# A graph-attention kernel: four weight tiles masked on GpSimd within the attention, and the first half of its output added to x there

## The chip, the core and the metric

The kernel runs on one core of a Trainium2 chip. A core has five engines that each work through a queue of their own in program order and wait for each other through semaphores: TensorE (PE in the profile, with PEld for its weight loads), VectorE (DVE), ScalarE (ACT), GpSimd (POOL) and SyncE (SP), which here only issues transfers. Matrix products are written to PSUM, everything else lies in SBUF. The metric is the device time of one execution in microseconds; the lower, the better.

## What is computed

Two graph layers over x of 16 batches x 1024 nodes x 256 channels, in fp32. Cut to what matters:

```python
# layer 0
h = relu(layernorm(x))
c_adj = mean(h, channels)                     # one number per node
diff = c_adj[:, None, :] - c_adj[:, :, None]
A = abs(abs(sigmoid(diff) - 0.5) - 0.5) * 2
W = adj * (A + A^T) / 2                       # 1024 x 1024 weights of each batch
q = relu((h^T W) * para)                      # the "graph" product
k, v = split(h @ kv_w)
x = x + softmax(q k^T * scale) v              # 4 heads of 64
# layer 1
h = relu(layernorm(x))
x = x + batchnorm(relu(batchnorm((A_hat h) @ W1.T + b1)) @ W2.T + b2)
```

A_hat is the adjacency matrix with unit diagonal added, normalized by its degrees. The batch norms run over all batches and nodes, so layer 1 is finished only when all 16 batches have passed its first product.

## The kernel before

The batches go one after another. While batch b is in its attention, the graph weights W of batch b+1 are begun; then the rest of them is made beside the graph product of b+1, then the values and keys of b+1 are made, and then the first product of layer 1 runs for batch b. That is one turn of the loop at L1440; the order of all instructions of PE, ACT, DVE, POOL and SP is the order in which the code issues them (`manual_schedule`, L1366), so each engine's queue is written by hand.

**Weights.** W of a batch is made in 8 tiles of 128 x 1024, one for 128 nodes. `differences` (L350) is two ScalarE instructions: the absolute difference (L353) and its tanh (L356). `masked` (L359) is one VectorE instruction (L361): (w - 1) times the tile of adj. The sign that this leaves is taken up in the scale of the queries. `weights` is both. The tiles live in a pool of five buffers (`w4`), tile 7 elsewhere.

**Attention** (`attention`, L791) goes in four steps: two halves g of 512 queries, and for each two pairs of heads. A step is `scores` (for 8 blocks m of keys: products into PSUM at L802, the exponential by ScalarE at L810, and the sums of exponentials by VectorE at L816, L822 and L825, with an odd and an even partial sum that L830 adds), then `partial` (VectorE: a transpose at L836 and a reduction at L844), then `values` (products at L852 and VectorE's transpose of their result at L865). In `scores`, the steps in `before_last` are issued ahead of L830; `hooks` puts `weights` of tiles 0 and 1 of the next batch there, in steps 0 and 1.

**Finishing a half** (`finish`, L870) has five parts: `collect` (ScalarE copies, L879), `invert` (VectorE: reciprocals of the sums, L885 to L888), `spread` (ScalarE copies, L894), `scale` (VectorE multiplies the half's output by them, L903, and 16 transfers on SP's queue put it into the order of x, L920) and `add` (VectorE adds it to x, L928). Half 0 is complete after step 1: its `collect` stands within step 2, `invert` and `spread` ahead of L830 of step 2, `scale` behind `partial` of step 2. Its `add` and all five parts of half 1 are returned in a list, `left`, and issued later.

**The graph stage** (`graph_seven`, L501; for batch 1 `graph`, L385) makes the graph product of b+1. Tiles 0 and 1 are multiplied plainly (L514). Tiles 2 to 7 are taken in three pairs, by seven products of sums of blocks in place of eight products (L575, `m1` to `m_7`), whose sums VectorE makes (`make_t1` to `make_t4`, L555 to L568). The stage begins with `differences` of tiles 2, 3 and 4, `masked` of 2 and 3, and `collect` and `invert` of the half 1 of batch b; masks 4 to 7 follow between the products. The add of half 0 (`add0`) stands behind the last sums, at L660, and the layer norm of the first half of x (`norm.stats(0, 4)`) behind it. The add of half 1 (`add1`, L746) comes in the values and keys stage.

In the first turn `between` (L1460) issues the list, with the add of half 0 behind tile 2's mask. In the last turn there is no next batch: `left[:3]` (the add, `collect`, `invert`) follows the attention at L1545, ahead of the first product of layer 1 for batch 14, which multiplies blocks of A_hat by h and by sums of blocks of h that VectorE makes at L995 to L998 (`sums_of_h`).

Of the kernel before, what the change touches and what calls it, by code (L numbers as in the profile page):

```python
# [10 lines left out]
F32 = mybir.dt.float32  # L11
AF = mybir.ActivationFunctionType
# [17 lines left out]
def fast_path(  # L30
# [145 lines left out]
    with ExitStack() as stage:  # L176
# [173 lines left out]
        def differences(b, c, w=None):  # L350
            if w is None:
                w = w4.tile([P, N], F32, tag="w4", name=f"f_w_{b}_{c}")
            nc.scalar.activation(  # L353
                w, rows[b], AF.Abs, bias=cols[b][:, c : c + 1], scale=0.5 / C
            )
            nc.scalar.activation(w, w, AF.Tanh)  # L356
            ws[b, c] = w

        def masked(b, c):  # L359
            w = ws[b, c]  # L360
            nc.vector.scalar_tensor_tensor(w, w, 1.0, adj_t[c], ALU.subtract, ALU.mult)  # L361
# [139 lines left out]
        def graph_seven(b, left, norm, load_more, last):  # L501
# [2 lines left out]


            gps = [ps_s.tile([P, N], F32, tag="s", name=f"f_gps_{b}_{d}") for d in range(CC)]
            add0, collect, invert, spread, scale, add1 = left
            h = hs[b]

            def plain(c):  # L510
# [91 lines left out]
            def m_7(n):  # L602
                one(m7, s3[n], t3[n], n, False, True)

            differences(b, 2)
            differences(b, 3)
            differences(b, 4)
            masked(b, 2)
            masked(b, 3)
            collect()  # L610
            invert()
            masked(b, 4)
# [44 lines left out]
            for n in range(PAIRS):  # L657
                m5(n)
            nc.scalar.copy(room[:, 1], x)
            add0()  # L660
            norm.stats(0, 4)
            norm.invert(0, 4)
            nc.vector.tensor_add(room[:, 2], room[:, 2], m7)
# [124 lines left out]
                todo.insert(0, late)  # L788
            return (qT, kT, v), todo

        def attention(b, qT, kT, v, hooks):  # L791

            steps = [(g, pair) for g in range(NH) for pair in range(HEADS // 2)]
            p_of, acc_of, odd_of, oT_of, o_of, red_of = {}, {}, {}, {}, {}, {}

            def scores(s, within=None, before_last=()):
                g, pair = steps[s]
                for m in range(NC):
                    ps = ps_s.tile([P, 2, 512], F32, tag="s", name=f"f_s_{b}_{s}_{m}")
                    for e in range(2):  # L800
                        rows_e = slice(e * HD, (e + 1) * HD)
                        nc.tensor.matmul(  # L802
                            ps[:, e, :],
                            kT[rows_e, pair, ts(m, P)],
                            qT[rows_e, pair, ts(g, 512)],
                            start=True,
                            stop=True,
                        )
                    p = pp.tile([P, 2, 512], F32, tag="p", name=f"f_p_{b}_{s}_{m}")
                    nc.scalar.activation(p, ps, AF.Exp)  # L810
                    p_of[s, m] = p
                    if m == 1:
                        acc = pp.tile(
                            [P, 2, 512], F32, tag="acc", name=f"f_acc_{b}_{s}", bufs=2
                        )
                        nc.vector.tensor_add(acc, p_of[s, 0], p)  # L816
                        acc_of[s] = acc
                    elif m == 3:
                        odd = ow.tile([P, 2, 16, 32], F32, tag="sums", name=f"f_sums_{b}_{s}")
                        odd_of[s] = odd  # L820
                        flat = odd.rearrange("p e j i -> p e (j i)")
                        nc.vector.tensor_add(flat, p_of[s, 2], p)  # L822
                    elif m > 3:
                        to = flat if m % 2 else acc_of[s]
                        nc.vector.tensor_add(to, to, p)  # L825
                    if m == 5 and within:
                        within()
                for step in before_last:
                    step()
                nc.vector.tensor_add(acc_of[s], acc_of[s], flat)  # L830

            def partial(s):

# [102 lines left out]
            for i in range(len(steps)):  # L936
                scores(
                    i,
                    collect if i == 2 else None,
                    [*hooks.get(i, ()), *([invert, spread] if i == 2 else [])],  # L940
                )
                partial(i)
                if i == 2:
                    scale()
                values(i)
            return [add] + finish(1)

# [416 lines left out]
        with tc.manual_schedule(engines={ENG.PE, ENG.Activation, ENG.DVE, ENG.Pool, ENG.SP}):  # L1366
# [72 lines left out]
            diagonal()  # L1439
            for b in range(B):  # L1440

                hooks = {}
                if b + 1 < B:
                    for c in range(2):
                        hooks.setdefault(c, []).append(lambda c=c: weights(b + 1, c))
                    if b == 0:
                        for m in range(NC):
                            hooks.setdefault(m // 2, []).append(lambda m=m: column_sums(m))
                        hooks[3].append(roots)
                else:  # L1450
                    hooks[0] = [lambda norm=norm: norm.relu(4, NC, False)]
                    w2n = lasting.tile([P, CC, F1], F32, tag="w2n", name="f_w2n")
                    nc.sync.dma_start(w2n, W2.rearrange("(c p) f -> p c f", p=P))
                left = attention(b, *qkv, hooks)

                def more(c):
                    return lambda: weights(b + 1, c)
# [1 line left out]
                norm = Norm(xr[b], f"b{b}")  # L1459
                between = {  # L1460
                    0: [
                        lambda: turn_h(b + 1), more(2), left[0], left[1], left[2], more(3),
                        left[3], left[4], more(4),
                    ],
                    1: [more(5)],
                    2: [more(6), lambda: norm.stats(0, 4)],
                    3: [more(7)],
                    4: [left[5], lambda: norm.stats(4, NC), norm.invert],
                    6: [lambda: norm.relu(0, 4)],
                    "late": [lambda: norm.relu(4, 6), lambda: norm.relu(6, NC)],  # L1470
                    8: [lambda: leave(b), lambda: arrive(b + 2)],
# [22 lines left out]
                if b + 2 < B:  # L1494
                    made = None
                    if b > 0:
                        made = sums_of_h(b, norm.h)
                        todo.pop(0)()
                    linear1_all(
                        b,  # L1500
                        norm.h,
                        thirds,
                        lambda: ([step() for step in todo], prepare_start(b + 2)),
                        lambda: (prepare_end(b + 2), pair_sums(b + 2, 0, 2)),
                        lambda: (prepare_row(b + 2), again(b + 1)),
                        turning=lambda: (pair_sums(b + 2, 2, 3), turn_h_aside(b + 2)),
                        made=made,
                    )
                elif b + 1 < B:
                    kept_h = norm.h  # L1510
                    again(b + 1)
                else:

                    w2T = lasting.tile([P, FC, C], F32, tag="w2T", name="f_w2T")

                    def first():
                        norm.stats(0, 4)
                        norm.invert(0, 4)
                        left[3]()
                        left[4]()  # L1520

                    def second():
                        norm.shifts(0, 4)
                        norm.relu(0, 4, False)

                    def third():
                        left[5]()
                        norm.stats(4, NC)
                        norm.invert(4, NC)
                        for n, (pool, tag) in enumerate(((ps_o, "o"), (ps_t, "t"))):  # L1530
                            ps = pool.tile([P, 2, CC, P], F32, tag=tag, name=f"f_w2ps_{n}")
                            for d in range(2):
                                for f in range(CC):
                                    nc.tensor.transpose(
                                        ps[:, d, f, :], w2n[:, f, ts(2 * n + d, P)], ident
                                    )
                            nc.scalar.copy(
                                w2T[:, 2 * n : 2 * n + 2, :].rearrange("p d c -> p (d c)"),
                                ps.rearrange("p d f q -> p (d f q)"),
                            )  # L1540
                        norm.shifts(4, NC)
                        norm.relu(4, NC, False)
                        leave(b)

                    for step in left[:3]:  # L1545
                        step()
                    thirds = load_thirds(b)
                    def nothing():
                        pass

                    made = []
                    linear1_all(
                        b - 1,
                        kept_h,
                        thirds,
                        first,
                        second,
                        third,
                        lambda: made.extend(sums_of_h(b, norm.h)),
                    )  # L1560
                    linear1_all(b, norm.h, thirds, nothing, nothing, nothing, made=made)
# [882 lines left out]
```

## Time and profile before

| | |
|---|---|
| time, median of 3 runs | 2384.4 us (2383.52 to 2384.42) |
| the profiled execution's own time | 2382.97 us |
| its span in the profile | 2381.1 us |
| TensorE's granted clock, mean | 0.995 |
| one batch in the middle (850.9 to 981.2 us) | 130.3 us |
| of it: attention; graph stage; values and keys; layer 1 | 56.3; 25.1; 12.9; 36.0 us |
| VectorE: mask of a tile (L361); add of a half (L928) | 1.21; 1.22 us |
| ScalarE: difference (L353); tanh (L356) | 1.16; 1.06 us |
| GpSimd: busy over the span | 175.1 us (7%) |

The span is the time from the first to the last instruction in the profile. An engine's row of the timeline gives start and length of an instruction, its line in the kernel, the tile that it writes and the tiles that it reads, and in brackets how long the engine had been idle before it and what ended that. Instructions of one engine can overlap a little at their ends: a VectorE addition of 1.22 us is followed by the next one 1.14 us after its start. Times in a trace are those of one execution, and sums made from them are held against its span.

### The profile page before, as it was taken

The numbers are of one execution on the slowest core, as the hardware profiler recorded it, in microseconds if no ns is written. First come the engines' busy times: TensorE is split into PE (matmuls) and PEld (weight loads), VectorE is DVE, ScalarE is ACT, GpSimd is POOL, SyncE is SP. The second block draws the span as 40 slices with busy tenths as digits, with TensorE's granted clock in tenths as the row PEclk, the third lists the DMA queues.
The fourth block names the chain that finished last, engine by engine and source line by source line (L and its number), as shares of the span: only waits on it lengthen the run. The fifth ranks groups of instructions, "written<-read, shape, count | busy, mean of one in ns | idle before, by whom it ended". The sixth has DMA issues, their size and how long they took to land.

```text
span 2381.1 us, 25131 instructions
## 1 busy us (share of the span) xinstructions
PE 2343.5 (98%) x8286; PEld 1037.3 (44%) x8286; DVE 1989.6 (84%) x2866; ACT 1352.6 (57%) x2002; POOL 175.1 (7%) x253
## 2 busy tenths in 40 slices
PE   8999999999999999999999999999999999999996
PEld 4443444434343434444343434344444434444444
DVE  6888989797989899897979798998979798757766
ACT  6846556464746555565647374555555575346654
POOL 2030010101010000101010100001010100000000
PEclk9999999999999999999999999999999999999998
DMA  5043433432342424334333414243433321355569
GB/s 194 8 145 93 147 119 129 137 122 91 97 160 68 167 93 169 97 129 137 124 98 110 146 62 169 89 172 93 146 120 127 114 92 53 114 203 188 175 238 381
DMA packets 178651, 316.40 MB, mean 133 GB/s; under 512 B 33616, under 2 KB 117072, under 8 KB 178512
## 3 DMA queue, kind: packets, MB, share of 16 engines
q1 hardware_dynamic: 164176, 271.18, 33.7%
q0 software_dynamic: 9728, 26.76, 3.8%
q10 hardware_dynamic: 4608, 16.78, 1.7%
q8 instruction: 67, 1.10, 0.2%
q14 instruction: 72, 0.59, 0.1%
HBM read 198.71 MB, written 97.05 MB: 124 GB/s over the span
## 4 chain that ended last, share of the span: by engine, by line
PE 97%; DVE 1%; DMA 1%; ACT 0%; issue 0%; SPq 0%; DVEq 0%; ACTq 0%; POOLq 0%; POOL 0%
PE f_s L802 19%; PE f_o L852 19%; PE f_aps L1011 16%; PE f_zps L1118 6%; PE f_gps L575 6%; PE f_gpsx L575 5%; PE f_gps L514 4%; PE f_zx L1661 4%; PE f_zm L1661 3%; PE f_gps L404 2%; PE f_kpsx L712 2%; PE f_vpsx L717 2%; PE f_vps L717 2%; PE f_kps L712 1%; PE f_z2ps L1599 1%; PE f_outps L1884 1%
## 5 line engine op out<-in xcount | busy, mean ns | idle before, releaser
L810 ACT ACTIVATE f_p<-f_s 128x1024 f32<-128x1024 f32 x512 | 477.5, 1048 | 189.2 <-PE f_s L802 189.1
L802 PE MATMUL f_s<-f_qT,f_kT 64*128 64x512 f32 x2048 | 457.3, 596 | 0.1
L852 PE MATMUL f_o<-f_p,f_v 128*64 128x512 f32 x2048 | 453.6, 595 | 0.0
L802 PEld LDWEIGHTS f_s<-f_qT,f_kT 64*128 64x128 f32 x2048 | 190.2, 185 | 264.8 <-ACT f_p L810 117.9
L852 PEld LDWEIGHTS f_o<-f_p,f_v 128*64 128x64 f32 x2048 | 141.4, 137 | 304.3 <-issue 265.4
L353 ACT ACTIVATE f_w<-f_row,f_col 128x1024 f32<-128x1024 f32 x127 | 147.0, 1157 | 40.0 <-PE f_gps L514 26.8
L825 DVE TENSOR_TENSOR f_acc<-f_acc,f_p 128x1024 f32<-128x1024 f32 x128 | 155.9, 1218 | 4.5 <-ACT f_p L810 4.5
L361 DVE SCALAR_TENSOR_TENSOR f_w<-f_w,f_adj 128x1024 f32<-128x1024 f32 x127 | 152.8, 1213 | 7.5 <-ACT f_w L356 7.2
L825 DVE TENSOR_TENSOR f_sums<-f_sums,f_p 128x1024 f32<-128x1024 f32 x128 | 155.8, 1217 | 0.0
L260 POOL TENSOR_TENSOR f_rstd_b<-f_var_b,f_mhalf 128x4 f32<-128x4 f32 (+1 forms) x31 | 33.1, 1069 | 1483.0 <-DVE f_var_b L259 1483.0
L356 ACT ACTIVATE f_w<-f_w 128x1024 f32<-128x1024 f32 x127 | 134.4, 1058 | 4.0
L1011 PE MATMUL f_aps<-f_ahatT,f_hs 128*128 128x512 f32 x256 | 115.1, 592 | 0.0
L1011 PE MATMUL f_aps<-f_ahatT,f_h_b 128*128 128x512 f32 x256 | 112.7, 593 | 0.0
L1011 PE MATMUL f_aps<-f_t,f_hs 128*128 128x512 f32 x256 | 112.5, 592 | 0.0
L816 DVE TENSOR_TENSOR f_acc<-f_p,f_p 128x1024 f32<-128x1024 f32 x64 | 76.9, 1201 | 27.6 <-ACT f_p L810 27.5
L514 PE MATMUL f_gps<-f_w,f_h_a 128*128 128x512 f32 x224 | 99.9, 599 | 0.0
L822 DVE TENSOR_TENSOR f_sums<-f_p,f_p 128x1024 f32<-128x1024 f32 x64 | 78.3, 1223 | 21.8 <-ACT f_p L810 21.8
L281 ACT ACTIVATE f_h_a<-f_x,f_shift_a,f_rstd_a 128x256 f32<-128x256 f32 x126 | 73.8, 587 | 38.5 <-DVE f_shift_a L266 38.5
L836 DVE STREAM_TRANSPOSE f_sums<-f_acc 128x1024 f32<-128x1024 f32 x64 | 79.7, 1245 | 2.2
L281 ACT ACTIVATE f_h_b<-f_x,f_shift_b,f_rstd_b 128x256 f32<-128x256 f32 x128 | 69.3, 595 | 21.5 <-DVE f_shift_b L266 21.5
L575 PE MATMUL f_gps<-f_w,f_h_a 128*128 128x512 f32 x168 | 81.2, 592 | 0.0
L1141 ACT ACTIVATE f_z<-f_zps,f_b 128x512 f32<-128x512 f32 x60 | 38.0, 683 | 75.3 <-PE f_zps L1118 75.3
(285 smaller groups left out, 3754.0 us busy)
## 6 DMA issues: line engine op xcount, KB each, us to landing
f_t<-ft SPq DMA_DIRECT2D x84, 512.0 KB, 11.1
fz<-f_z SPq DMA_DIRECT2D x64, 512.0 KB, 9.7
f_x<-in_x_dram SPq DMA_DIRECT2D x31, 1024.0 KB, 7.0
f_zb<-fz SPq DMA_DIRECT2D x42, 512.0 KB, 3.9
f_att<-f_oT SPq DMA_DIRECT2D x512, 32.0 KB, 1.9
fx<-f_x SPq DMA_DIRECT2D x16, 1024.0 KB, 4.4
fhT<-f_hQ POOLq DMA_DIRECT2D x112, 128.0 KB, 2.9
f_hT<-fhT SPq DMA_DIRECT2D x28, 512.0 KB, 5.9
```

The lines of the kernel that those rows point to most:

```text
L281: nc.scalar.activation(self.h[:, c, :], self.xt[:, c, :], AF.Relu, bias=self.shift[:, c : c + 1], scale=self.rstd[:, c : c + 1], accum_out ...
L353: nc.scalar.activation(w, rows[b], AF.Abs, bias=cols[b][:, c : c + 1], scale=0.5 / C)
L361: nc.vector.scalar_tensor_tensor(w, w, 1.0, adj_t[c], ALU.subtract, ALU.mult)
L514: nc.tensor.matmul(gps[d][:, ts(g, 512)], h[:, c, ts(d, P)], w[:, ts(g, 512)], start=(c == 0), stop=(c == PLAIN - 1),)
L575: nc.tensor.matmul(ps, left, right, start=fresh and n == 0, stop=(n == PAIRS - 1), skip_group_check=more,)
L802: nc.tensor.matmul(ps[:, e, :], kT[rows_e, pair, ts(m, P)], qT[rows_e, pair, ts(g, 512)], start=True, stop=True,)
L810: nc.scalar.activation(p, ps, AF.Exp)
L825: nc.vector.tensor_add(to, to, p)
L852: nc.tensor.matmul(o_of[s][e * HD : (e + 1) * HD, :], v[:, m, ts(2 * pair + e, HD)], p[:, e, :], start=(m == 0), stop=(m == NC - 1),)
L1011: nc.tensor.matmul(ps, left[:, m, :], right(m), start=not more and m == 0, stop=(m == KH - 1), skip_group_check=more,)
L1118: nc.tensor.matmul(ps[i], left[:, ts(i, P)], right, start=not more, stop=True, skip_group_check=more,)
L1661: nc.tensor.matmul(ps, left[:, m, :], right[:, m, :], start=start and m == 0, stop=(m == 1), skip_group_check=not start,)
```

## The change

Three things are done, all in the attention and the stages behind it.

From the second turn on, `differences` of tiles 0 to 3 of the next batch are issued in steps 0 to 3 of the attention (before: `weights` of 0 and 1 in steps 0 and 1, and `differences` of 2 and 3 in the graph stage). Their masks are made by a new function, `masked_aside`, which is issued behind L830 of the same step: VectorE sets a column to -1, ScalarE adds it to the tile, and GpSimd multiplies the tile by that of adj. `masked(b, 2)` and `masked(b, 3)` go from the graph stage. The first turn keeps its way of making tiles 0 and 1.

In every turn, the add of half 0 is issued in step 3 of the attention, ahead of L830 and of that step's hooks. It goes from the graph stage, from `between` and from the end of the last turn.

```diff
+        def masked_aside(b, c):
+            now = small.tile([P, 1], F32, tag="now", name=f"f_now_{b}_{c}")
+            nc.vector.memset(now, -1.0)
+            w = ws[b, c]
+            nc.scalar.activation(w, w, AF.Identity, bias=now)
+            nc.gpsimd.tensor_mul(w, w, adj_t[c])
...
-            add0, collect, invert, spread, scale, add1 = left
+            collect, invert, spread, scale, add1 = left
...
-            differences(b, 2)
-            differences(b, 3)
             differences(b, 4)
-            masked(b, 2)
-            masked(b, 3)
             collect()
             invert()
             masked(b, 4)
...
             nc.scalar.copy(room[:, 1], x)
-            add0()
             norm.stats(0, 4)
...
-        def attention(b, qT, kT, v, hooks):
+        def attention(b, qT, kT, v, hooks, aside):
...
-            def scores(s, within=None, before_last=()):
+            def scores(s, within=None, before_last=(), after_last=()):
...
                 for step in before_last:
                     step()
                 nc.vector.tensor_add(acc_of[s], acc_of[s], flat)
+                for step in after_last:
+                    step()
...
                 scores(
                     i,
                     collect if i == 2 else None,
-                    [*hooks.get(i, ()), *([invert, spread] if i == 2 else [])],
+                    [
+                        *([add] if i == 3 else []),
+                        *hooks.get(i, ()),
+                        *([invert, spread] if i == 2 else []),
+                    ],
+                    aside.get(i, ()),
                 )
                 partial(i)
                 if i == 2:
                     scale()
                 values(i)
-            return [add] + finish(1)
+            return finish(1)
...
-                hooks = {}
+                hooks, aside = {}, {}
                 if b + 1 < B:
-                    for c in range(2):
-                        hooks.setdefault(c, []).append(lambda c=c: weights(b + 1, c))
+                    for c in range(2 if b == 0 else 4):
+                        if b == 0:
+                            hooks.setdefault(c, []).append(lambda c=c: weights(b + 1, c))
+                            continue
+                        hooks.setdefault(c, []).append(lambda c=c: differences(b + 1, c))
+                        aside[c] = [lambda c=c: masked_aside(b + 1, c)]
...
-                    for step in left[:3]:
+                    for step in left[:2]:
```

The other lines of the diff only renumber the entries of `left`. Nothing is computed differently in the end, and no transfer is added, removed or moved in SP's queue.

More of the change, by code (lines that the diff above doesn't have):

```diff
@@ L1453, in fast_path @@
                     nc.sync.dma_start(w2n, W2.rearrange("(c p) f -> p c f", p=P))
-                left = attention(b, *qkv, hooks)
+                left = attention(b, *qkv, hooks, aside)
                 def more(c):
@@ L1461, in fast_path @@
                     0: [
-                        lambda: turn_h(b + 1), more(2), left[0], left[1], left[2], more(3),
-                        left[3], left[4], more(4),
+                        lambda: turn_h(b + 1), more(2), left[0], left[1], more(3),
+                        left[2], left[3], more(4),
                     ],
@@ L1467, in fast_path @@
                     3: [more(7)],
-                    4: [left[5], lambda: norm.stats(4, NC), norm.invert],
+                    4: [left[4], lambda: norm.stats(4, NC), norm.invert],
                     6: [lambda: norm.relu(0, 4)],
@@ L1518, in first @@
                         norm.invert(0, 4)
+                        left[2]()
                         left[3]()
-                        left[4]()
                     def second():
@@ L1526, in third @@
                     def third():
-                        left[5]()
+                        left[4]()
                         norm.stats(4, NC)
```

## The prediction

> **What bounds the kernel now.** I read four views in this order: busy shares, the stages of one batch, TensorE's waits, and then the order in time around the change.
>
> ```profile
> PE 2343.5 (98%) x8286; PEld 1037.3 (44%) x8286; DVE 1989.6 (84%) x2866; ACT 1352.6 (57%) x2002; POOL 175.1 (7%) x253
> ```
>
> TensorE is busy 98% of the span. A share is an average, so the batch whose attention begins at 850.9 us is cut into attention, the graph stage of the next batch, its values and keys, and the linear layer. Columns: stretch, its length, busy time of PE, PEld, DVE, ACT and POOL (with instructions), granted clock, DMA share, GB/s.
>
> ```profile
> 850.92:907.26 56.34, 56.34 (x258) 20.76 (x257) 53.30 (x55) 41.33 (x50) 0.00 (x0) 1.00 0.21 65
> 907.26:932.34 25.08, 25.08 (x61) 11.04 (x59) 24.27 (x41) 10.62 (x17) 1.03 (x1) 1.00 0.79 279
> 932.34:945.20 12.86, 12.86 (x72) 8.97 (x71) 11.36 (x21) 7.32 (x14) 1.01 (x1) 1.00 0.29 94
> 945.20:981.20 36.00, 36.00 (x87) 15.63 (x85) 24.49 (x51) 14.34 (x31) 7.39 (x11) 1.00 0.38 110
> ```
>
> In all four PE's busy time equals the stretch, at full clock. VectorE is almost as full in the first two (53.3 of 56.3 and 24.3 of 25.1 us). TensorE's waits lie at the two ends of the program; the first and longest rows:
>
> ```profile
> PE f_adjps L1293 <- DMA f_adj<-in_adj_dram: 10.0, 1, 10.0
> PE f_outps L1884 <- ACT f_z L1864: 5.0, 2, 2.9
> ```
>
> L1293 is the start and L1884 the output. So work taken from VectorE in attention or the graph stage can win nothing: there is no gap in TensorE's row to close. What it can do is open one. The rows of VectorE and SP in order of time (start, length) show how near that is:
>
> ```profile
> 895.06 1.21 DVE L903 TENSOR_TENSOR f_oT<-f_oT,f_recs 128x1024 f32<-128x1024 f32 x1
> 896.30 10.77 SPq L920 DMA_DIRECT2D f_att<-f_oT  x16
> 904.01 1.23 DVE L830 TENSOR_TENSOR f_acc<-f_acc,f_sums 128x1024 f32<-128x1024 f32 x1
> 907.69 0.71 DVE L865 STREAM_TRANSPOSE f_oT<-f_o 128x512 f32<-128x512 f32 x1
> 911.84 1.21 DVE L361 SCALAR_TENSOR_TENSOR f_w<-f_w,f_adj 128x1024 f32<-128x1024 f32 x1
> 920.96 1.22 DVE L361 SCALAR_TENSOR_TENSOR f_w<-f_w,f_adj 128x1024 f32<-128x1024 f32 x1
> 922.39 0.19 PEld L575 LDWEIGHTS f_gps<-f_w,f_h_a 128*128 128x128 f32 x1 [0.24 <-DVE f_w L361]
> 925.48 1.21 DVE L928 TENSOR_TENSOR f_x<-f_x,f_att 128x1024 f32<-128x1024 f32 x1
> ```
>
> The reader is to see two things. First, the mask of tile 7 (920.96 to 922.18) ends 0.2 us before TensorE loads weights for the product that reads it (922.39), and from 917.4 to 925.5 VectorE has no pause. Whatever makes VectorE later than 0.2 us there is paid by TensorE one for one. Second, the half that is added to x at L928 arrives by 16 transfers issued after L903 (895.06). They fill SP's queue until 907.07, and page 6 gives 1.9 us from issue to landing, so the last, issued at 906.48, lands at 908.4: 13.3 us after L903 began. By the same reading of all 16 batches it is 12.7 to 14.0, mean 13.1.
>
> **The change, part by part.**
>
> *The add moves to step 3, ahead of L830.* L830 stands at 904.01, and the transfers land at 908.4. VectorE takes its queue in order, so it now stands still behind the add. The last batch shows what such a wait looks like, because there the add already follows attention directly:
>
> ```profile
> 2032.16 1.22 DVE L903 TENSOR_TENSOR f_oT<-f_oT,f_recs 128x1024 f32<-128x1024 f32 x1
> 2045.75 1.23 DVE L928 TENSOR_TENSOR f_x<-f_x,f_att 128x1024 f32<-128x1024 f32 x1 [0.27 <-issue]
> ```
>
> The add began 13.6 us after L903, with a landing at 13.2 in that batch; so I put it at the mean landing plus 0.3, 13.4 us after L903. Behind it on VectorE are L830, the new memset, the row sums' transpose and reduction, the transpose of step 3's output, the reciprocals and masks 4 to 7; behind those wait ScalarE's subtraction of tile 3, its differences 4 to 7, and TensorE.
>
> *GpSimd's product.* No row has it at 128x1024. The program's first POOL rows give a scale for contiguous tiles: a memset of 128x1 takes 0.10 us and of 128x128 0.20, so 0.79 ns per element and access; a select (one read, one write) of 128x128 takes 0.30, twice that. Two reads and a write: 0.1 + 1024 x 2.4 ns = 2.5 us, which I take, as the tiles are contiguous. Low end: VectorE's own 1.2 us (L361). High end: GpSimd's strided 128x128 products at L1333, 0.52 us undisturbed, times eight: 4.2 us.
>
> *What it does to VectorE.* Where both ran at the start of the program, VectorE's 128x128 operations of two SBUF tensors took 0.28 us when they began first and 0.6 when a GpSimd product was under way:
>
> ```profile
> 54.86 0.28 DVE L1094 TENSOR_TENSOR f_kvs<-f_kvw 128x128 f32<-128x128 f32 x1
> 55.06 0.60 DVE L1095 TENSOR_TENSOR f_kvs<-f_kvw,f_kvs 128x128 f32<-128x128 f32 x1
> 54.87 0.65 POOL L1334 TENSOR_TENSOR f_ahatT<-f_ahatT,f_ident 128x128 f32<-128x128 f32 x1
> ```
>
> So they wait for each other. The transposes and the reduction have one input and I let them run; L903 has two. In step 2 L830 ends at 892.63, memset 0.06 (the 128x8 row at L79), ScalarE's subtraction 1.06 (as L356), so GpSimd runs from 893.9 to 896.4 and L903 starts at 896.4 instead of 895.06. In steps 0 and 1 the products (865.2 to 867.7, 878.1 to 880.6) end before the next step's first add can start (868.1, 882.2): nothing. ScalarE ends its subtractions 1.0, 2.1 and 0.6 us before the next exponential of steps 1, 2 and 3 (866.18, 880.26, 894.41): hidden there, and paid beyond those margins.
>
> *The sum in one batch* (us). Add to x 896.4 + 13.4 = 909.8; L830 one spacing (1.14) later, 910.9; memset, transpose 912.25, reduction 913.5, ending 914.7; output's transpose 914.65. ScalarE: subtraction 912.25 to 913.3, differences of tile 4 to 915.45 (2.1), copies of the sums to 916.7 (1.24). VectorE: reciprocals from 916.7, mask 4 at 918.0 (1.3 later, as from 910.55 to 911.84 now). That is 6.2 later than 911.84, though masks 2 and 3 (2.3 us) are gone, for the copies and not the masks end last. All stays 6.2 late to mask 7, which ends at 928.4; TensorE's load, due at 922.39, is 6.0 late. Earlier waits (products of tiles 3 and 5, which need at most 4.4) are part of it. The transfers of the graph stage (907.80 on) wait for the reduction too, 6.9 us; the sums of h land 3.6 us later, near 918.3, 2.8 late for their first use at 915.5: also covered by the 6.0. After tile 7 the add is gone from VectorE (1.1 us less), so nothing more is lost.
>
> Fourteen batches go this way: 14 x 6.0 = 84. The first (no GpSimd) has the add's wait alone: L903 at 109.03, waits passed at 122.7, the transposes of h and mask 2 six us later (131.9), where TensorE wants tile 2 at 128.1: 3.8. In the last, the sums of h at L996 end at 2054.65 instead of 2049.6 and the product of them is due at 2050.9: 3.8. Gains: none, since TensorE has no gap. Together 92 on the span's 2381.1: 2473. The median lies 3.3 over that span: **2476 us**.
>
> Ends: with L903 not held up (a product of 1.2 us, or no contention) a batch loses 4.7, in all 73: 2458. With 4.2 us L903 starts at 898.1, a batch loses 7.7, in all 115: 2500.
>
> The Trainium skill ("GPSIMD Engine Reference", Performance versus the Vector engine) speaks against this edit: elementwise work on two tensors is about half as fast on GpSimd, 4497 ns for 2048 fp32 elements. An estimate from it is 2.25 us for 1024; the batch would lose 5.75 and the time be 2472; no run here has shown that row.
>
> **The rivals.**
>
> *Not slower.* One mechanism: the transfers land before VectorE reaches the add at 904.0, that is within 8.9 us of L903. Then the add is 1.2 us in a queue that loses 3.5 elsewhere, TensorE keeps its row full, and the time is 2384. For it: the 16 transfers are only 32 KB each, and before the change this add never waits for them in the batches with a graph stage (at 925.48 it follows its neighbour). Against: 16 of 16 batches land at 12.7 or later, and nothing in the change shortens them. That the change does not do what it says falls here too; but in the changed program's order the add does stand ahead of the final sum of step 3, with waits for eight transfer queues.
>
> *GpSimd costs nothing.* L903 starts at 895.1: 2458, as worked out. For it: GpSimd's 1 us power operations (L260) overlap VectorE's adds freely. Against: the 0.28 and 0.60 above.
>
> *TensorE also slows down.* The stalls (up to 2.3 us at a time for a product of 2.5 us, 3 for 4.2) might drop the clock. In the output stage the granted clock was 0.50 from 2320.7 for 3.3 us after idle stretches of 2.0 and 0.9 us, and from 2334.4 for 10 us after one of 2.9. Half the clock for 3.4 us costs 1.7, in 14 batches 24: 2500. Against: full matmuls stand between these stalls, short transposes in the output.
>
> The Trainium skill ("TensorE: Matmul & The Clock Gate", Part 1) says that a window of about 3.4 us of idling halves the clock. By that rule no stall here is long enough, and the sum stays 2476; the rows of the output stage, where 2.0 and 0.9 sufficed, are stricter.
>
> **How the numbers follow.** The sum as made 0.60; GpSimd free 0.18; slower clock or a dearer product 0.17; not slower 0.05. The range reaches from a little below the free case (landings at their earliest, 12.7: 14 x 0.4 less) nearly to the slow-clock case with a dear product (2500 + 24): 2450 to 2520. 0.2% (4.8 us) is about what a measurement of this kernel tells from none: slower 0.93, within 0.05, faster 0.02.
>
> **What would show it.** VectorE idle before the add in step 3, released by SP's transfers, 4 to 5 us in each of 16 batches; the add 13.4 us after L903; L903 started by GpSimd's end; TensorE waits in the graph stage on VectorE's masks, some 6 us a batch. If the add starts near 904, or TensorE's batches still last 130.3 us, this is wrong.

## The result, and the profile after

| | before | after |
|---|---|---|
| time, median of 6 runs | 2384.32 us (2383.52 to 2384.42) | 2468.8 us (2465.68 to 2472.03) |
| ratio, with its 95% interval | | 1.0356 [1.0342, 1.0369] |
| span of the profiled execution | 2381.1 us | 2469.7 us |
| one turn, mean of the 13 from the second to the fourteenth | 130.29 us | 135.60 us |

The change made the kernel 3.6% slower: inside the range that was forecast, 7 us under the forecast time. From the page of the changed kernel: the engines, and two groups of instructions (busy time, mean ns; idle time of the engine before them and what ended it).

```profile
PE 2373.7 (96%) x8286; PEld 1040.0 (42%) x8286; DVE 1944.8 (79%) x2866; ACT 1418.6 (57%) x2058; POOL 307.8 (12%) x309
...
L366 POOL TENSOR_TENSOR f_w<-f_w,f_adj 128x1024 f32<-128x1024 f32 x56 | 132.1, 2359 | 880.1 <-ACT f_w L365 880.1
...
L934 DVE TENSOR_TENSOR f_x<-f_x,f_att 128x1024 f32<-128x1024 f32 x32 | 39.1, 1221 | 74.6 <-DMA f_att<-f_oT 74.6
```

VectorE has 45 us less to do and the span is 88.6 us longer. A product on GpSimd takes 2.36 us. The last row is the new thing: VectorE stands still 74.6 us ahead of the add (L934 in the changed kernel), until transfers have landed. The four stages of the turn that begins at 884.9 us, in the columns shown before (length; PE, PEld, DVE, ACT, POOL; granted clock):

```profile
884.90:941.20 56.30, 56.30 (x258) 20.77 (x257) 49.07 (x53) 43.74 (x51) 7.07 (x3) 1.00 0.21 64
941.20:971.88 30.68, 26.30 (x60) 10.71 (x59) 25.21 (x42) 12.88 (x19) 3.40 (x2) 1.00 0.64 228
971.88:984.70 12.82, 12.82 (x72) 8.92 (x71) 11.36 (x21) 7.28 (x14) 1.01 (x1) 1.00 0.32 99
984.70:1020.70 36.00, 36.00 (x85) 15.65 (x83) 24.44 (x51) 14.40 (x31) 7.44 (x11) 1.00 0.38 110
```

Three stages are as long as before. The graph stage went from 25.1 to 30.7 us, and PE, which had no gap in it, is idle for 4.4. In order of time in this turn, rows of GpSimd, VectorE, SP and TensorE:

```profile
927.89 2.35 POOL L366 TENSOR_TENSOR f_w<-f_w,f_adj 128x1024 f32<-128x1024 f32 x1 [13.24 <-ACT f_w L365]
929.00 2.33 DVE L909 TENSOR_TENSOR f_oT<-f_oT,f_recs 128x1024 f32<-128x1024 f32 x1
931.36 10.78 SPq L926 DMA_DIRECT2D f_att<-f_oT  x16
943.73 1.23 DVE L934 TENSOR_TENSOR f_x<-f_x,f_att 128x1024 f32<-128x1024 f32 x1 [4.99 <-DMA f_att<-f_oT]
950.65 0.41 DVE L891 TENSOR_REDUCE f_rec<-f_parts 32x64 f32<-32x256 f32 x1 [1.41 <-ACT f_parts L885]
961.06 1.22 DVE L370 SCALAR_TENSOR_TENSOR f_w<-f_w,f_adj 128x1024 f32<-128x1024 f32 x1
962.34 1.13 PE L584 MATMUL f_gps<-f_w,f_h_a 128*128 128x512 f32 x2 [1.38 <-DVE f_w L370]
```

The multiplication that releases the transfers (L903 before, L909 now) takes 2.33 us instead of 1.21, as GpSimd's product is under way until 930.24. The transfers go out from 931.36, the add starts at 943.73, the reciprocals wait for ScalarE's copies, and mask 7 starts at 961.06. Counted from the start of step 3's scores (893.17 before, 927.11 now) mask 7 is at 33.95 instead of 27.79: 6.2 us late. The product that reads tile 7 waits for it.

```profile
PE f_gps L584 <- DVE f_w L370: 20.6, 23, 1.4
PE f_gps L584 <- DMA f_gs<-fgs: 18.1, 14, 1.5
...
PE f_gps L584 <- DVE f_v L565: 6.4, 13, 0.7
PE f_gps L584 <- POOL f_w L366: 5.6, 6, 1.3
PE f_gps L413 <- DVE f_w L370: 3.7, 1, 3.7
```

These are TensorE's waits in the graph stages (total us, times, longest); none of them is in the profile before. They name four different releasers (tile 7's mask stands twice), and each of these can be called the cause. The experiments tell which one sets the end.

### The profile page after: what moved, and what is told of

Its sections match the earlier page's. It is cut to its first block, busy times and chain, and to the rows that moved or that the text cites. A ratio compares the mean times of both kernels' runs of the same rounds, so it can differ in the third digit from the quotient of the medians.

```text
span 2469.7 us, 25122 instructions
## 1 busy us (share of the span) xinstructions
PE 2373.7 (96%) x8286; PEld 1040.0 (42%) x8286; DVE 1944.8 (79%) x2866; ACT 1418.6 (57%) x2058; POOL 307.8 (12%) x309
## 4 chain that ended last, share of the span: by engine, by line
PE 69%; DVE 13%; ACT 7%; SPq 5%; issue 4%; DMA 2%; DVEq 0%; ACTq 0%; POOLq 0%; POOL 0%
PE f_aps L1022 15%; PE f_s L806 11%; PE f_o L858 10%; PE f_zps L1129 6%; SPq L926 5%; PE f_zx L1676 4%; ACT f_p L814 4%; PE f_gpsx L584 3%; PE f_zm L1676 3%; PE f_gps L584 3%; PE f_kpsx L716 2%; PE f_vpsx L721 2%; DVE f_w L370 2%; PE f_gps L413 2%; PE f_vps L721 2%
## 5 line engine op out<-in xcount | busy, mean ns | idle before, releaser
L366 POOL TENSOR_TENSOR f_w<-f_w,f_adj 128x1024 f32<-128x1024 f32 x56 | 132.1, 2359 | 880.1 <-ACT f_w L365 880.1
L365 ACT ACTIVATE f_w<-f_w,f_now 128x1024 f32<-128x1024 f32 x56 | 64.3, 1148 | 161.3 <-DVE f_now L363 161.3
L1022 PE MATMUL f_aps<-f_t,f_hs 128*128 128x512 f32 x256 | 115.6, 605 | 3.1 <-issue 3.1
L1022 PE MATMUL f_aps<-f_ahatT,f_hs 128*128 128x512 f32 x256 | 115.1, 592 | 0.0
L1022 PE MATMUL f_aps<-f_ahatT,f_h_b 128*128 128x512 f32 x256 | 112.7, 593 | 0.0
L934 DVE TENSOR_TENSOR f_x<-f_x,f_att 128x1024 f32<-128x1024 f32 x32 | 39.1, 1221 | 74.6 <-DMA f_att<-f_oT 74.6
L370 DVE SCALAR_TENSOR_TENSOR f_w<-f_w,f_adj 128x1024 f32<-128x1024 f32 x71 | 86.1, 1214 | 3.8 <-ACT f_w L356 3.8
```

Source lines behind the costliest of these rows:

```text
L366: nc.gpsimd.tensor_mul(w, w, adj_t[c])
L1022: nc.tensor.matmul(ps, left[:, m, :], right(m), start=not more and m == 0, stop=(m == KH - 1), skip_group_check=more,)
```

## The experiments

Times are medians; the ratios are against the kernel before, measured alongside.

| run | what differs | time | ratio | mean turn |
|---|---|---|---|---|
| e1_add_back | changed kernel, add back in the graph stage | 2383.17 us | 0.9997 [0.9987, 1.0007] | 130.27 us |
| e2_add_only | kernel before, only the add moved | 2464.0 | 1.0339 [1.0321, 1.0356] | 135.27 |
| e3_add_behind | changed kernel, add behind step 3's values | 2384.2 | 1.0001 [0.9992, 1.0011] | 130.32 |
| e4_two_queues | changed kernel, transfers on two queues | 2398.05 | 1.0060 [1.0043, 1.0076] | 131.32 |
| e5_tile2_later | changed kernel, tile 2 on GpSimd in step 3 | 2452.78 | 1.0290 [1.0273, 1.0307] | 134.47 |
| e6_constant | changed kernel, column of -1 set once | 2450.29 | 1.0281 [1.0264, 1.0298] | 134.21 |
| e7_more_vector | kernel before, 3 extra VectorE operations | 2406.05 | 1.0093 [1.0077, 1.0110] | 131.91 |
| e8_still_more_vector | kernel before, 8 extra | 2457.88 | 1.0310 [1.0293, 1.0328] | 135.55 |

### Which half of the change: e1 and e2

```diff
# e1, on the changed kernel (and the indices of left)
-                        *([add] if i == 3 else []),
...
-            return finish(1)
+            return [add] + finish(1)
...
+            add0()
             norm.stats(0, 4)
```

> The changed kernel with the add of half 0 put back into the graph stage; GpSimd still masks tiles 0 to 3. Theory (the add's wait for its transfers is the loss): step 3 ends 0.8 us later, because L903 is still held by GpSimd, but masks 2 and 3 are gone, so the reciprocals begin 17.4 us after step 3's start as before the change; 2384 to 2387 us. Rival (GpSimd's product and ScalarE's subtraction make tiles 2 and 3 late): half of the 84 us or more stays, 2425 or above.

2383.17 us: no measurable difference from the kernel before, though GpSimd still makes its 56 products. Rows of this run, in the turn that begins at 851.05: the reduction of step 3, the reciprocals, masks 4 and 7.

```profile
907.52 1.22 DVE L851 TENSOR_REDUCE f_red<-f_sums 128x32 f32<-128x1024 f32 x1
910.77 0.41 DVE L892 TENSOR_REDUCE f_rec<-f_parts 32x64 f32<-32x256 f32 x1 [1.42 <-ACT f_parts L886]
912.07 1.21 DVE L370 SCALAR_TENSOR_TENSOR f_w<-f_w,f_adj 128x1024 f32<-128x1024 f32 x1
...
921.18 1.22 DVE L370 SCALAR_TENSOR_TENSOR f_w<-f_w,f_adj 128x1024 f32<-128x1024 f32 x1
```

The two masks that left VectorE leave it idle for 1.42 us ahead of the reciprocals, and mask 7 is 0.09 us later in its turn than before. So this half of the change is free, and it gains nothing: TensorE had no gap.

e2 is the other half: the lines on `add` of the change's diff alone, on the kernel before.

> The kernel before with only the add moved ahead of the final sum of step 3; VectorE masks as before. Theory: L903 is not held, so the add starts 1.3 us earlier than in the changed kernel, but masks 2 and 3 (2.3 us) stand behind it again: mask 4 is 5.6 us late instead of 6.2, TensorE loses 4.7 to 5.4 us a batch and about 11 in the first and last turn: 2455 to 2470. Rival (GpSimd and ScalarE are the cause): at most 20 us slower than before, 2405 or below.

2464.0 us. The moved add alone makes nearly the whole loss, 80 of 84 us, and GpSimd's masks are out as its cause; what they add on top of the moved add, e5 and e6 measure.

### What of the add: e3 and e4

```diff
# e3, on the changed kernel
-                        *([add] if i == 3 else []),
...
                 values(i)
+            add()
             return finish(1)
```

> The changed kernel with the add issued behind the last step's values instead of ahead of its final sum, so only the reciprocals and masks stand behind it. Theory (what stands behind the add is what is lost): transposes and sums of step 3 are no longer held; the add ends 17.8 us after step 3's start, when the copies of the sums end (17.4), mask 4 is 0.4 late, TensorE loses up to 0.3 a batch: 2384 to 2392. Rival (an add this early costs wherever it stands): 2440 or above.

2384.2 us: the add can stand in front of the graph stage at no cost that can be told from zero. It starts at 909.70 in this row, 0.7 us after VectorE became free, and the reciprocals follow at 910.84. Counted from the turn's start (850.69) they begin at 60.15 us, 0.43 later than in e1 (59.72); that is less than the margin of 0.57 us that e7 and e8 measure below.

```profile
909.70 1.23 DVE L934 TENSOR_TENSOR f_x<-f_x,f_att 128x1024 f32<-128x1024 f32 x1 [0.70 <-issue]
910.84 0.40 DVE L891 TENSOR_REDUCE f_rec<-f_parts 32x64 f32<-32x256 f32 x1
```

So the add is not too early in itself. What costs is that the final sum of step 3, its transpose and its reduction stand behind it in VectorE's queue, and ScalarE's copies wait for that reduction.

```diff
# e4, on the changed kernel, in scale
-                            nc.sync.dma_start(
+                            queue = nc.gpsimd if g == 0 and j % 2 else nc.sync
+                            queue.dma_start(
```

> The changed kernel with half 0's 16 transfers issued alternately on SP's and GpSimd's queues. Theory (the wait is SP's 0.64 us per issue): the last of 8 is issued 4.5 us after the first and lands 1.9 later, before VectorE reaches the add; what is left is the add's own 1.1 us and the copies behind it, about 1.1 us a batch: 2390 to 2410. Rival (the wait is of the data's way or of something else on VectorE): 2450 or above.

```profile
903.49 6.02 SPq L927 DMA_DIRECT2D f_att<-f_oT  x8
903.76 4.29 POOL L927 DMA_DIRECT2D f_att<-f_oT  x8 [1.38 <-DVE f_oT L909]
911.49 1.23 DVE L935 TENSOR_TENSOR f_x<-f_x,f_att 128x1024 f32<-128x1024 f32 x1 [0.62 <-DMA f_att<-f_oT]
```

Rows of SP, GpSimd and VectorE. SP's issues take 6.0 us instead of 10.8, VectorE waits 0.62 us instead of 4.99, and 71 of the 84 us are gone. The way from the last issue to its landing is still 1.8 to 2.1 us (3.3 in one of the 16 turns). So the wait was the issuing of 16 transfers one after another on one queue, not the way of the data.

### How large each term is: e5 to e8

```diff
# e5, on the changed kernel
+                    if b > 0:
+                        aside["in 3"] = aside.pop(2)[0]
...
-                    collect if i == 2 else None,
+                    collect if i == 2 else aside.get("in 3") if i == 3 else None,
```

> The changed kernel with tile 2's subtraction and GpSimd product issued behind the sixth exponential of step 3 instead of at the end of step 2, so that GpSimd is idle when L903 starts. Theory (L903 is held by GpSimd's product, and all that follows moves with it): L903 takes 1.2 us again instead of 2.3, the add starts 1.1 us earlier, each of 14 batches gains 1.1: 15 us faster than the changed kernel, 2450 to 2457. Rival (something other than the transfers' landing ends last): no gain, 2465 to 2472.

2452.78 us, 16 less than the changed kernel. L909 takes 1.21 us again. The hold only moved, to an addition of step 3, where VectorE would have waited for the transfers anyway:

```profile
920.64 1.21 DVE L909 TENSOR_TENSOR f_oT<-f_oT,f_recs 128x1024 f32<-128x1024 f32 x1
...
929.43 2.58 DVE L829 TENSOR_TENSOR f_acc<-f_acc,f_p 128x1024 f32<-128x1024 f32 x1 [2.20 <-ACT f_p L814]
...
928.57 2.37 POOL L366 TENSOR_TENSOR f_w<-f_w,f_adj 128x1024 f32<-128x1024 f32 x1 [22.28 <-ACT f_w L365]
```

```diff
# e6, on the changed kernel
-            now = small.tile([P, 1], F32, tag="now", name=f"f_now_{b}_{c}")
-            nc.vector.memset(now, -1.0)
...
-            nc.scalar.activation(w, w, AF.Identity, bias=now)
+            nc.scalar.activation(w, w, AF.Identity, bias=minus)
# minus is a constant tile, set to -1 once at the start
```

> The changed kernel with the column of -1 set once at the start of the program, so that ScalarE's subtraction of tile 3 no longer waits for VectorE behind the add, and tile 3's mask and tile 4's differences are done early. Theory (behind the add the row sums end last, then ScalarE's copies, not tile 3's mask): the copies start when the sums are there, 0.8 us earlier; 8 to 12 us faster than the changed kernel, 2456 to 2462. Rival (ScalarE's wait of 8.4 us and tile 3's late mask are the loss): 2430 or below.

2450.29 us: the rival is out, but the gain was 18.5 us and not 8 to 12. Rows of ScalarE and of L909:

```profile
919.13 1.15 ACT L365 ACTIVATE f_w<-f_w,f_minus 128x1024 f32<-128x1024 f32 x1
...
941.54 1.25 ACT L885 COPY f_parts<-f_red 32x64 f32<-32x64 f32 x4 [7.37 <-DVE f_red L850]
922.02 1.78 DVE L909 TENSOR_TENSOR f_oT<-f_oT,f_recs 128x1024 f32<-128x1024 f32 x1
```

The expected part is in the second row: the copies now wait for the reduction alone. What was overlooked is in the others. In step 2 the subtraction need not wait for the memset either (0.6 us), so GpSimd's product starts earlier and L909 is held 0.57 us instead of 1.12.

For e7 and e8 the first `make_t3(0)` of the graph stage is written four and nine times in the kernel before:

```diff
+            for _ in range(4):
-            make_t3(0)
+                make_t3(0)
             make_t1(0)
```

> The kernel before with three extra, repeated VectorE subtractions (L556, 0.6 us each, same result) in the graph stage ahead of mask 5. Nothing else changes. Theory: VectorE is 1.8 us later at mask 7, and TensorE loses what goes beyond its margin there: with the margin of the prediction (0.2 us) 1.6 in 14 batches, 2406; with 0.6 us (to the product's start and not its weight load) 1.2, 2401. Rival (VectorE's lateness is absorbed): 2384.

> As the run with three extra subtractions, with eight: 4.8 us later at mask 7. Theory, one for one beyond the margin: with 0.2 us 4.6 a batch, 2448; with 0.6 us 4.2, 2443. The step from three to eight is 42 us by both. Rival (absorbed in part): a step of less than 30.

```profile
921.39 2.85 DVE L556 TENSOR_TENSOR f_v<-f_w,f_w 128x512 f32<-128x512 f32 x4
...
931.55 1.22 DVE L361 SCALAR_TENSOR_TENSOR f_w<-f_w,f_adj 128x1024 f32<-128x1024 f32 x1
```

2406.05 us is the number expected for a margin of 0.2, but for another reason, which the rows of e7 show: repeats on one tile follow each other every 0.73 us and not every 0.6. In its turn mask 7 is 2.18 us later than before and the turn 1.62 longer (131.89 for 130.27); in e8 it is 5.81 later and the turn 5.24 longer. Both leave a margin of 0.57 us, and beyond it TensorE pays one for one. The step from e7 to e8, 52 us, is close to 5 x 0.73 x 14 = 51.

### One line through all of it

From the start of L903 (or its line there) to the start of the add, mean over the same 13 turns, against what a turn lost:

| run | L903 to the add | turn lost | difference |
|---|---|---|---|
| after | 14.44 us | 5.32 us | 9.12 us |
| e4_two_queues | 10.14 | 1.03 | 9.10 |
| e5_tile2_later | 13.30 | 4.18 | 9.12 |
| e6_constant | 13.78 | 3.92 | 9.86 |
| e2_add_only | 13.38 | 4.98 | 8.40 |

In the changed kernel, with two queues or with tile 2 later, a turn loses what this interval exceeds 9.1 us. With the constant column the copies begin 0.75 us sooner and the limit is 9.9; with masks 2 and 3 on VectorE it is 8.4. The same holds turn by turn: in the changed kernel the interval runs from 13.86 (turn of 135.01 us) to 15.40 (136.55). One turn of the 13 lies 0.3 us off this line (13.91, 135.33).

## Why the prediction was right, point by point

*No gap to close.* Right: e1 makes four of the eight masks of a graph stage with GpSimd and gains nothing that can be told from zero.

*The add waits for its transfers, and what stands behind it is late.* Right: e2 has the loss without GpSimd. e3 is free of it, since only the reciprocals and masks stand behind the add there, and e4 of most of it, since the wait is gone. The add was put at 14.7 us after L903's old start and came at 14.4.

*GpSimd's product, 2.5 us, and L903 held until its end.* Right: 2.36 us, and L909 takes 1.12 us longer. e5 prices the hold at 16 us; the forecast had 14 x 1.3 = 18. The Trainium skill ("SBUF — State Buffer", Who interferes with whom) states that a VectorE instruction with two SBUF inputs contends with a GpSimd one that reads SBUF, and that their shared ports are an exclusive lock; the 2.33 and 2.58 us above agree, each ending about 1.1 us after the product beside it. The estimate of 2.25 us for the product, scaled from the skill's 4497 ns for 2048 elements ("GPSIMD Engine Reference", Performance versus the Vector engine), is 5% under the 2.36 measured.

*Masks 4 to 7 are 6.2 us late.* Right to 0.1 us in the turn shown, which is one of the longer ones; the mean of the fourteen is 5.9, as the add comes 0.3 us earlier than it was put.

*TensorE loses all but 0.2 us of that.* This step failed by size: "The mask of tile 7 ends 0.2 us before TensorE loads weights for the product that reads it". The 0.2 us are the margin of the weight load (922.39), and a late load need not make its product late. The product starts only at 922.81, 0.63 us behind the mask's end. Rows of the kernel before and of the changed kernel (where PE's row stands above, at 962.34):

```profile
922.81 1.02 PE L575 MATMUL f_gps<-f_w,f_h_a 128*128 128x512 f32 x2
...
962.34 0.30 PEld L584 LDWEIGHTS f_gps<-f_w,f_h_a 128*128 128x128 f32 x2 [2.21 <-DVE f_w L370]
```

In the changed kernel the load waits for the mask, and its product starts with it, not 0.4 us behind. So those 0.4 us are slack that a late load uses up first. e7 and e8 measure a margin of 0.57 us, and the changed kernel has the same: its mask 7 is 5.86 us late in the mean and a turn loses 5.3. Together with the earlier add this makes 5.3 us a turn instead of 6.0: fourteen graph stages lost 74 us and not 84.

*First and last turn, 3.8 us each.* This was priced too low. The waits were 3.75 and 3.14 us, but the turns cost 7.1 and 6.8. TensorE rows of the changed kernel's first and last turn, and the stretches behind the waits (length, PE busy and so on, granted clock third from the right):

```profile
132.71 6.75 PE L413 MATMUL f_gps<-f_w,f_h_a 128*128 128x512 f32 x8 [3.75 <-DVE f_w L370]
2136.39 8.85 PE L1022 MATMUL f_aps<-f_t,f_hs 128*128 128x512 f32 x13 [3.14 <-issue]
...
132.20:138.80 6.60, 6.09 (x7) 2.52 (x8) 5.16 (x8) 5.11 (x9) 6.60 (x14) 0.50 0.32 81
2135.80:2142.40 6.60, 6.00 (x7) 2.52 (x8) 4.06 (x13) 0.00 (x0) 1.01 (x1) 0.50 0.06 24
```

The clock is at half for 6.8 us at each wait, which costs 3.4. Other runs show the price: in e5's first turn (a wait of 3.67 us) the clock was at half for 3.4 us only, and the turn lost 5.4; in e6's last turn (3.11 us) it stayed at full, and TensorE ended the products of L1022 3.4 us late, against 6.4 in the changed kernel. That is the third rival, at work in two places. The prediction wrote "no stall here is long enough", with the stalls of up to 2.3 us of the middle turns in view and not its own 3.8 at the two ends. So 74 + 7.1 + 6.8 and 0.6 from a later start make the 88.6 us between the two spans, where the forecast had 92. That the sum came so close is partly luck: the middle turns were priced 10 us too high and the two ends 6 too low. The profiled execution was one of the longer ones (2471.5 us against a median of 2468.8).

*The rivals.* Not slower: out, no turn's transfers landed in time. GpSimd free: out, by e5. A slower clock: in five of the 13 middle turns the clock was at half for 3.4 us, and it cost at most 0.3 us there. It is not what the loss is made of: in e2 and e6 the clock stayed at full in all 13, and a turn lost 5.0 and 3.9 us all the same. The turn from 1155.7 us, with the stretch of its graph stage at half clock and two of its PE rows:

```profile
1224.40:1227.70 3.30, 3.30 (x5) 1.30 (x4) 3.27 (x6) 3.24 (x4) 0.00 (x0) 0.50 0.98 382
...
1225.44 1.91 PE L584 MATMUL f_gpsx<-f_w,f_h_a 128*128 128x512 f32 x2
1232.39 1.12 PE L584 MATMUL f_gps<-f_w,f_h_a 128*128 128x512 f32 x2 [0.49 <-DVE f_w L370]
```

Two products take 1.91 us there instead of 1.02, but the wait for mask 7 is 0.49 us and not 1.38: TensorE spends in slow products what it would have waited. The turn took 135.05 us, and one with the same interval to the add (13.9) and no half clock took 135.05.

## What to carry to other kernels

Before an instruction is moved forward in an in-order queue, look up when its last input lands, here 1.9 us behind the last of 16 issues at 0.64 us each, and what stands behind it; an add that is needed late goes behind the work that is needed soon. Work taken from an engine whose consumer has no gaps is worth nothing, however full that engine is. A margin is read at the product whose late start costs time, not at its weight load, which here ran 0.4 us ahead of need.

## What the runs showed of the hardware that was not expected

A wait of TensorE of 3.1 or 3.8 us left the clock at half for 6.8 us in the changed kernel, though one of 3.1 in e6 did not. In five middle turns of the changed kernel waits of at most 1.5 us each, 1.8 to 2.4 us in the 5 us before, were enough for 3.4 us at half; the turn from 884.9 us idled 2.5 us in such a stretch and kept the full clock. The Trainium skill ("TensorE: Matmul & The Clock Gate", Part 1) names a window of idling of about 3.4 us; by these rows a partly idle one suffices, and the measurement decides. Whether the clock drops differs between like turns, but in the middle ones it cost at most 0.3 us here.

The 16 issues on SP's queue do not always take the same: landings after L903 spread by 1.3 us among turns of the kernel before, where nothing waited for them. In the changed kernel the spread shows up in the turns one for one, and its runs scatter over 6.4 us where those of the kernel before lie within 0.9.
